# Row maxima of a softmax laid along all partitions by DMA and ScalarE instead of a TensorE transpose

## The chip, the core and the metric

The kernel runs on one core of a Trainium2 chip, in one launch. The metric is the device time of that core in microseconds, in several runs; beside it stands one execution taken by the hardware profiler. All data is float32.

## The reference, cut to what matters

```python
mod = (silu(c) @ wmod).reshape(8, 6, 1, 256)          # sa, ca, ga, sb, cb, gb by batch
h = layernorm(x) * (1 + ca) + sa                      # x: 8 batches x 1024 rows x 256
scores = einsum('nsd,ntd->nst', h * w_lhs, h * w_rhs) # 8 x 1024 x 1024
x = x + ga * (softmax(scores, axis=2) @ h)
h = layernorm(x) * (1 + cb) + sb
x = x + gb * (relu(h @ W1 + b1) @ W2 + b2)            # 256 -> 1024 -> 256
```

So each of eight batches has an attention over 1024 rows, whose softmax takes the maximum of every score row, and then a two-layer network on each row.

## The kernel before, in words

A batch's 1024 rows are eight tiles of 128 (P); i counts them, and a half g is four of them. The loop at the bottom runs over batches b and tiles i. One turn of it holds work of three places: the scores of the tile `ahead`, two tiles on; the softmax of the tile `late`, one tile on; and the product of tile i with the values, or a part of a product of two tiles. In the same turn stands a piece of the network of the batch before (half g = i // 4) and of the preparation of the next. `pin` ties each engine's instructions to the order in which the program emits them, DMAs included. So no scheduler moves anything, and each engine and each DMA queue runs strictly through its list.

Scores are symmetric in a way that the kernel uses: tile i computes only the columns from its own on (`direct`, L412), and ScalarE copies them from PSUM to the buffer sc (L419). The rest of the lower rows comes by `mirror`: VectorE turns blocks of 32x32 (L435), and `move` sends them to DRAM by four DMAs (D_m, L306) and reads them back by one (sc<-D_m, L309). Other transposes go the same way by `move`: the normalized rows of the next batch (D_a and X_a), of the network (D_f and X_f), and the network's result (D_y and Y). All of these are issued by SyncE, whose queue is in program order. A read stands there until its four writes have landed. The attention's and the network's products are done with seven half-size products for eight, which gives the sums on GpSimd and VectorE around them.

The transposed score tile is what the value product needs: columns of sc, with the score row along the free axis. So the maximum of each of the tile's 128 rows, which `row_max` leaves in one number per partition (m, L463), must stand along the free axis on every partition, as 128 x 128 numbers. `max_turn` does that by a TensorE transpose of m broadcast to 128 columns, into PSUM (pm, L468). `subtract` on VectorE (L475) takes pm from the columns, and `exponent` on ScalarE (L484) gives pT, the weights of the product. sc has one buffer, so a new batch's first scores wait for the last subtraction of the old one.

The network's first layer is made of pairs of column blocks, c = 0 to 3 for each half, two pairs in each turn with i % 4 < 2. `pair_products` (helper L726) writes pa, pb and pc, and ScalarE copies pa to kept (L747). Then `pair_sums` adds on VectorE, and `pair_last` writes a last product over the low half of pa (L778, through L726 too), adds it on VectorE (L779) and adds kept on GpSimd (L780). `pair_relu` is ScalarE's (L789, L790).

`max_turn` is called between matmuls, so that its small transpose stands inside another stage's stream. The turn i = 4 emits the next batch's second half before its maximum:

```python
                pair_last(fb, fg, c + 1)
                if i == 4:
                    if b + 1 < B:
                        prepare_blocks(b + 1, 1)
                        xg_times(b + 1, 1)
                    weights(*late)
                if ahead and ahead != extra:
                    row_max(*ahead)
```

Of the kernel before, what the change touches and what calls it, by code (L numbers as in the profile page):

```python
# [11 lines left out]
F32 = mybir.dt.float32  # L12
# [5 lines left out]
P = 128  # L18
# [6 lines left out]
def adaln_block_kernel(  # L25
# [13 lines left out]
    nc = tc.nc  # L39
    B, S, D = x.shape  # L40
    INTER = W1.shape[1]
    NT = S // P
# [3 lines left out]
    TH = HALF // P  # L46
    H2 = HALF // 2
    NH = NI // 2
    V = 32
    NV = P // V  # L50
    DX = D + 4

    const = ctx.enter_context(tc.tile_pool(name="const", bufs=1))
    two = ctx.enter_context(tc.tile_pool(name="two", bufs=2))
    work = ctx.enter_context(tc.tile_pool(name="work", bufs=3))
# [38 lines left out]
    early_d = two.tile([P, 4, D], F32, tag="X", name="early_d", bufs=1)  # L94
# [7 lines left out]
    def load_x0(q, queue):  # L102
# [11 lines left out]
        out=wv[ND : 2 * ND, :], in_=w_rhs.rearrange("a b (k p) -> (a b k) p", p=P)  # L114
# [19 lines left out]
    ident = const.tile([P, P], F32, name="ident")  # L134
# [5 lines left out]
    def warm(n):  # L140
# [9 lines left out]
            name=nc.get_next_instruction_name(),  # L150
# [6 lines left out]
    NC_ = ND * B  # L157
# [1 line left out]
        nc.tensor.transpose(pt_c[:, ts(k, B)], c_sb[:, ts(k, P)], ident[:B, :B])  # L159
    scT = const.tile([P, ND, B], F32, name="scT")  # L160
    scf = scT.rearrange("p k b -> p (k b)")
    den = const.tile([P, NC_], F32, name="den")
    nc.scalar.activation(den, pt_c[:, :NC_], AF.Exp, scale=-1.0)

    def silu():
# [90 lines left out]
    def prepare_start(b):  # L256
        xg_t[b] = two.tile([P, NT, DX], F32, tag="xg", name=f"xg_{b}")
        nc.gpsimd.memset(xg_t[b][:, :, D : D + 1], 1.0)
# [89 lines left out]
    def prepare_turn(b, g, vector=True):  # L348

        xg, pts = xg_t[b], []  # L350
        lT = lT_t[b, g] = two.tile([P, ND, HALF], F32, tag="lT", name=f"lT_{b}_{g}", bufs=2)
        rT = rT_t[b, g] = two.tile([P, ND, HALF], F32, tag="rT", name=f"rT_{b}_{g}", bufs=2)
        rows = lambda T, k: T[:, k, :].rearrange("p (t a v) -> p t a v", a=NV, v=V)
        for k in range(ND):
            if b > 0:
                pt = pre[b, g][:, k]
            else:
                pt = ps_t.tile([P, HALF], F32, tag="t", name=f"pth_{b}_{g}_{k}")
                for j in range(TH):
                    nc.tensor.transpose(pt[:, ts(j, P)], xg[:, g * TH + j, ts(k, P)], ident)  # L360
                pt = pt.rearrange("p (t a v) -> p t a v", a=NV, v=V)
            pts.append(pt)

        def left(k):
            nc.vector.tensor_scalar(
                rows(lT, k), pts[k], side_col(0, 0, k, b), side_col(0, 1, k, b),
                ALU.mult, ALU.add,
            )


        for k in range(ND):
            if vector:
                left(k)
            q = ND - 1 - k if vector else k
            nc.scalar.activation(
                rows(rT, q), pts[q], AF.Identity,
                scale=side_col(1, 0, q, b), bias=side_col(1, 1, q, b),
            )
        return left
# [13 lines left out]
    def score_row(b, i):  # L393
        if b == 0:
            return first_scores()[:, i].rearrange("p (n v) -> p n v", v=V)
        return sc_t[b].rearrange("p i a j v -> p j (i a) v")[:, i]
# [62 lines left out]
    max_t, pT_t = {}, {}  # L459

    def row_max(b, i):
        m = work.tile([P, 1], F32, tag="m", name=f"m_{b}_{i}")
        nc.vector.tensor_reduce(m, score_row(b, i), AX.XY, ALU.max)  # L463
        max_t[b, i] = m

    def max_turn(b, i):
        pm = ps_t.tile([P, HALF], F32, tag="t", name=f"pm_{b}_{i}")
        nc.tensor.transpose(pm[:, :P], max_t.pop((b, i)).to_broadcast([P, P]), ident)  # L468
        pT_t[b, i] = pm

    def subtract(b, i):

        pm = pT_t.pop((b, i))
        pT = work.tile([P, NT, P], F32, tag="pT", name=f"pT_{b}_{i}")
        nc.vector.tensor_tensor(  # L475
            pT.rearrange("p j (a v) -> p j a v", v=V),
            score_columns(b, i),
            pm[:, :P].rearrange("p (j a v) -> p j a v", j=1, v=V).to_broadcast([P, NT, NV, V]),
            ALU.subtract,
        )  # L480
        pT_t[b, i] = pT

    def exponent(b, i):
        nc.scalar.activation(pT_t[b, i], pT_t[b, i], AF.Exp)  # L484
# [35 lines left out]


    XS = D - P + 1
    tsum = const.tile([P, 4, TH, P + 4], F32, name="tsum")
    nc.gpsimd.memset(tsum[:, 1, :, P : P + 1], 1.0)

    def right_sums(b, which):

        xg = xg_t[b]
        b11, b12 = xg[:, 0:TH, P:D], xg[:, 0:TH, 0:P]
        b21, b22 = xg[:, TH:NT, P:D], xg[:, TH:NT, 0:P]  # L530
        t = [tsum[:, n, :, 0:P] for n in range(4)]
        ins = [(b12, b11), (b22, t[0]), (b22, b12), (t[1], b21)]
        for n in which:
            nc.gpsimd.tensor_tensor(t[n], *ins[n], ALU.subtract)
# [4 lines left out]
    def pair_begin(b, i, between=None):  # L539

        W = work.tile([P, 2, D + 4], F32, tag="W", name=f"W_{b}_{i}", bufs=1)
        pp = ps_a.tile([P, HALF], F32, tag="a", name=f"pp_{b}_{i}")
        one, other = halves(pT_t[b, i])
        rows = slice(P, P + XS)
        for out, lhs, h in (
            (pp[:, 0:XS], one, 0), (pp[:, XS : 2 * XS], other, 1)
        ):
            for t in range(TH):
                nc.tensor.matmul(  # L549
                    out, lhsT=lhs[:, t, :], rhs=xg_t[b][:, h * TH + t, P : P + XS],  # L550
                    start=(t == 0), stop=(t == TH - 1),
                )
            if between and h == 0:
                between()
        nc.scalar.copy(W[:, 1, rows], pp[:, 0:XS])
        two_t[b, i] = W, pp
# [22 lines left out]
    def pair_end(b, i):  # L579

        (s2, s4), (s3, a22) = halves(pT_t.pop((b, i))), halves(pT_t.pop((b, i + 1)))
        s1 = two_t.pop("s1")
        pq = ps_a.tile([P, HALF], F32, tag="a", name=f"pq_{b}_{i}")
        pr = ps_a.tile([P, HALF], F32, tag="a", name=f"pr_{b}_{i}")
        for out, lhs, rhs in (
            (pr[:, P : 2 * P], s1, tsum[:, 0, :, 0:P]),
            (pq[:, XS : XS + P], a22, tsum[:, 3, :, 0:P]),
            (pr[:, 2 * P : 3 * P], s3, tsum[:, 2, :, 0:P]),
            (pq[:, 0:XS], s2, tsum[:, 1, :, 0:XS]),
            (pr[:, 0:P], s4, xg_t[b][:, TH:NT, 0:P]),  # L590
        ):
            for t in range(TH):
                nc.tensor.matmul(  # L593
                    out, lhsT=lhs[:, t, :], rhs=rhs[:, t, :],
                    start=(t == 0), stop=(t == TH - 1),
                )
        two_t[b, i] = two_t[b, i][0], pq, pr
# [27 lines left out]
    def pair_stats(b, i):  # L625
        two_t.pop((b, i))
        for t in (i, i + 1):
            stats(mvb_of(b, t // TH), t % TH, x_tile(b, t), f"b{b}_{t}")
# [8 lines left out]
    def spare():  # L637
        if queue:
            queue.popleft()()
# [369 lines left out]
    def first_rows():  # L1009

        pr = ps_a.tile([P, HALF], F32, tag="a", name="prow")
        nc.tensor.matmul(
            pr[:, :HALF],
            lhsT=ident[:, 0:1].to_broadcast([P, P]),
            rhs=early_c[:, 0:2, :].rearrange("b j d -> b (j d)"),
            start=True,
            stop=True,
        )
        return pr
# [17 lines left out]
    pr = first_rows()  # L1037
# [106 lines left out]
    def weights(b, i):  # L1144
        subtract(b, i)
        exponent(b, i)

    last_exponent = (0, 1)
    late = None
    for b in range(B):  # L1150
        for i in range(NT):
# [8 lines left out]
            if (b, i) == (0, NT - 2):  # L1160

                prepare_turn(1, 1)
                product(b, i)
                direct(*ahead)
                exponent(*last_exponent)
                product_out(b, i)
                mirror(*ahead)
                early(b, i)
                for _ in range(4):
                    spare()  # L1170
                norms(b, i)
                row_max(*ahead)
                late, last_exponent = ahead, None
                continue
            if ahead and ahead != (0, 2):
                direct(*ahead)
            if b == 0:
# [37 lines left out]
            if first:  # L1215
# [28 lines left out]
                if (b, i) == (1, 0):  # L1244
                    exponent(*late)
                    late = None
# [41 lines left out]
            else:  # L1288
# [5 lines left out]
                if i == 2:  # L1294
                    left_sums(b, 1)
                elif i == 3:
                    pair_begin(b, i, turn_max)
                elif i == 6:
                    pair_begin(b, i, lambda: (max_turn(*late), weights(*late)))
                elif not ahead:  # L1300

                    pair_end(b, i - 1)
                    pair_out(b, i - 1)
                    pair_stats(b, i - 1)
# [64 lines left out]
            late = ahead if ahead != extra else None  # L1369
# [7 lines left out]
    b = B - 1  # L1377
# [74 lines left out]
```

## Time and profile before

| | before |
|---|---|
| time, median of 3 runs | 757.19 us (756.47 to 757.96) |
| profiled execution, its own time | 756.93 us |
| its span, first to last instruction | 755.1 us |
| busy: TensorE | 749.1 us, 99% |
| busy: VectorE | 574.9 us, 76% |
| busy: GpSimd | 570.9 us, 76% |
| busy: ScalarE | 374.9 us, 50% |
| DMA packets, bytes | 106213, 95.21 MB |
| maxima turned by TensorE (L468) | 64 times |

The page's first parts give each engine's busy time and the chain of work that ended last. Groups of instructions stand by line, engine and operation, with what ended the idle time before them. The timeline gives single instructions with start and duration in us: "PE" is a matmul on TensorE, "PEld" its weight load, "DVE" VectorE, "ACT" ScalarE, "POOL" GpSimd, and "SPq" a DMA that SyncE issues. The idle time before an instruction and what ended it stand in square brackets. L468 is line 468 of the kernel. A steady batch takes about 90.4 us.

### The profile page before, as it was taken

What the parts mean: (1) busy time and instruction counts of PE and PEld (TensorE: products, weight loads), DVE (VectorE), ACT (ScalarE), POOL (GpSimd) and SP (SyncE); (2) the same over time, 40 slices, a digit from 0 to 9 for tenths busy, and PEclk for the clock granted to TensorE, in tenths of its full rate; (3) what the DMA queues carried; (4) which work ended last, traced back from release to release, by engine and by line L of the source; (5) the groups of instructions that cost most, each with busy time, mean ns of one, the idle gap of its engine ahead of it and who ended that gap; (6) DMA issues with size and microseconds to landing.
All of it is one profiled execution on the core that took longest, in us unless ns stands there. A gap on an engine that the chain in (4) does not pass through costs nothing.

```text
span 755.1 us, 11883 instructions
## 1 busy us (share of the span) xinstructions
PE 749.1 (99%) x3876; PEld 623.4 (83%) x3876; DVE 574.9 (76%) x1259; ACT 374.9 (50%) x688; POOL 570.9 (76%) x658
## 2 busy tenths in 40 slices
PE   8999999999999999999999999999999999999998
PEld 4686889788897888888888878988889788888887
DVE  7787879778796879968878688876889777685632
ACT  4554646635375454745546444563546535252521
POOL 3762796878968798788877699777996888669741
PEclk9999999999999999999999999999999999999999
DMA  9033442455443453445534555245553354133220
GB/s 308 16 112 98 131 133 74 135 178 152 127 120 123 153 153 110 147 118 158 164 99 119 153 154 161 74 127 172 155 152 85 119 166 133 50 91 126 84 85 28
DMA packets 106213, 95.21 MB, mean 126 GB/s; under 512 B 29700, under 2 KB 98848, under 8 KB 106152
## 3 DMA queue, kind: packets, MB, share of 16 engines
q1 hardware_dynamic: 98408, 85.81, 38.6%
q10 hardware_dynamic: 7744, 8.65, 3.7%
q8 instruction: 30, 0.49, 0.3%
q14 instruction: 31, 0.25, 0.1%
HBM read 50.62 MB, written 43.81 MB: 125 GB/s over the span
## 4 chain that ended last, share of the span: by engine, by line
PE 96%; DMA 1%; DVE 1%; ACT 1%; issue 0%
PE psc L412 16%; PE pa L726 11%; PE po L501 10%; PE pr L593 7%; PE pb L726 7%; PE pc L726 7%; PE yc L806 6%; PE ya L806 6%; PE yb L806 6%; PE pq L593 5%; PE pp L549 5%; PE py L916 4%; PE yd L806 3%; DMA wm<-in_L_wmod_dram 1%; PE pm L468 1%; PE pmr L194 0%
## 5 line engine op out<-in xcount | busy, mean ns | idle before, releaser
L412 PE MATMUL psc<-rT,lT 128*128 128x512 f32 (+3 forms) x384 | 134.8, 487 | 0.0
L780 POOL TENSOR_TENSOR f<-f,kept 128x512 f32<-128x512 f32 x64 | 81.5, 1274 | 42.8 <-DVE f L779 20.1
L419 ACT COPY sc<-psc 128x512 f32<-128x512 f32 (+3 forms) x96 | 44.7, 476 | 119.9 <-PE psc L412 113.0
L484 ACT ACTIVATE pT<-pT 128x1024 f32<-128x1024 f32 x64 | 67.6, 1056 | 70.6 <-DVE pT L475 70.5
L475 DVE TENSOR_TENSOR pT<-sc,pm 128x1024 f32<-128x1024 f32 x64 | 77.3, 1208 | 29.3 <-PE pm L468 13.7
L412 PEld LDWEIGHTS psc<-rT,lT 128*128 128x128 f32 x384 | 66.4, 191 | 37.2 <-issue 25.6
L501 PE MATMUL po<-xg,pT 128*128 128x257 f32 x352 | 80.6, 380 | 0.0
L463 DVE TENSOR_REDUCE m<-sc 128x1 f32<-128x1024 f32 x64 | 77.4, 1209 | 2.2 <-ACT sc L419 1.8
L501 PEld LDWEIGHTS po<-xg,pT 128*128 128x128 f32 x352 | 66.2, 190 | 10.0 <-issue 0.7
L747 ACT COPY kept<-pa 128x512 f32<-128x512 f32 x64 | 37.4, 584 | 69.3 <-PE pa L726 69.1
L726 PE MATMUL pb<-hs,w1s 128*128 128x256 f32 x256 | 65.9, 380 | 0.1
L726 PE MATMUL pc<-hT,w 128*128 128x256 f32 x256 | 65.7, 379 | 0.0
L880 POOL TENSOR_TENSOR x<-x,Y 128x512 f32<-128x512 f32 x28 | 35.1, 1276 | 29.3 <-DMA Y<-D_y 29.3
L789 ACT ACTIVATE f<-f 128x512 f32<-128x512 f32 x64 | 39.8, 622 | 34.7 <-POOL f L780 34.7
L642 POOL TENSOR_TENSOR x<-x,rows 128x256 f32<-128x256 f32 x64 | 44.8, 732 | 13.8 <-ACT rows L1022 10.6
L726 PEld LDWEIGHTS pb<-hs,w1s 128*128 128x128 f32 x256 | 48.5, 190 | 7.3 <-DVE f L765 0.8
L726 PEld LDWEIGHTS pc<-hT,w 128*128 128x128 f32 x256 | 48.6, 190 | 6.7
L806 PE MATMUL yc<-f,w2s 128*128 128x256 f32 x224 | 51.3, 379 | 0.0
L435 DVE STREAM_TRANSPOSE Tm<-sc 128x896 f32<-128x896 f32 (+6 forms) x49 | 34.3, 701 | 20.3 <-ACT sc L419 19.6
L806 PEld LDWEIGHTS yc<-f,w2s 128*128 128x128 f32 x224 | 41.5, 190 | 8.1 <-issue 2.9
L549 PEld LDWEIGHTS pp<-xg,pT 128*128 128x128 f32 x336 | 41.9, 192 | 5.1 <-DVE st_b L241 1.4
L799 POOL TENSOR_TENSOR ft<-f 128x256 f32<-128x256 f32 x56 | 40.8, 729 | 6.8 <-ACT f L790 6.8
(166 smaller groups left out, 1821.1 us busy)
## 6 DMA issues: line engine op xcount, KB each, us to landing
D_f<-T_f SPq DMA_DIRECT2D x60, 128.0 KB, 2.5
X_f<-D_f SPq DMA_DIRECT2D x15, 512.0 KB, 3.7
D_a<-T_a SPq DMA_DIRECT2D x56, 128.0 KB, 2.8
D_y<-T_y SPq DMA_DIRECT2D x56, 128.0 KB, 2.9
Y<-D_y SPq DMA_DIRECT2D x14, 512.0 KB, 3.4
out_dram<-x SPq DMA_DIRECT2D x14, 512.0 KB, 4.4
X_a<-D_a SPq DMA_DIRECT2D x13, 512.0 KB, 3.4
x<-in_L_attn_x_dram ACTq DMA_DIRECT2D x12, 512.0 KB, 3.4
```

What stands on the lines that cost most here:

```text
L412: nc.tensor.matmul(psc[:, : hi - lo], lhsT=lT_t[b, i // TH][:, k, ts(i % TH, P)], rhs=rT_t[b, n][:, k, lo - n * HALF : HALF], start=(k == ...
L419: nc.scalar.copy(score_row(b, i)[:, lo // V : hi // V, :], psc[:, : hi - lo].rearrange("p (n v) -> p n v", v=V),)
L463: nc.vector.tensor_reduce(m, score_row(b, i), AX.XY, ALU.max)
L475: nc.vector.tensor_tensor(pT.rearrange("p j (a v) -> p j a v", v=V), score_columns(b, i), pm[:, :P].rearrange("p (j a v) -> p j a v", j=1, ...
L484: nc.scalar.activation(pT_t[b, i], pT_t[b, i], AF.Exp)
L501: nc.tensor.matmul(po[:, : D + 1], lhsT=pT[:, t, :], rhs=xg_t[b][:, t, 0 : D + 1], start=(t == 0), stop=(t == NT - 1),)
L549: nc.tensor.matmul(out, lhsT=lhs[:, t, :], rhs=xg_t[b][:, h * TH + t, P : P + XS], start=(t == 0), stop=(t == TH - 1),)
L593: nc.tensor.matmul(out, lhsT=lhs[:, t, :], rhs=rhs[:, t, :], start=(t == 0), stop=(t == TH - 1),)
L642: queue.append(lambda: nc.gpsimd.tensor_tensor(out, in0, row, op))
L726: nc.tensor.matmul(out, lhsT=lhsT, rhs=rhs, start=True, stop=True)
L780: nc.gpsimd.tensor_tensor(f[:, c::NH, hi], f[:, c::NH, hi], kept[:, None, hi].to_broadcast([P, 2, H2]), ALU.add,)
L806: nc.tensor.matmul(out, lhsT=lhs(c), rhs=rhs(c), start=(c == 0), stop=(c == NH - 1))
```

## The change

From the second batch on (b > 0), the maxima are spread without TensorE. Right after the maximum, `row_max` has VectorE turn m, broadcast to 32 columns, in blocks of 32x32 (mb, 128 x 32): the rows 0, 32, 64 and 96 of mb then hold 32 maxima each. Four DMAs issued by SyncE copy these rows, each from one partition to all 128, into mt (128 x 4 x 32, in SBUF). `max_turn` is a ScalarE copy of mt into the PSUM tile pm. mb and mt have one buffer each. For tile 7 the call of `max_turn` moves from inside `pair_begin` to the start of the turn i = 6, ahead of the next scores. To make room, xg's rows become two numbers shorter (DX), den lies in an early buffer, and the four parts of tsum are packed closer.

```diff
-    DX = D + 4
+    DX = D + 2
...
-    den = const.tile([P, NC_], F32, name="den")
+    den = early_d[:, 2, P : P + NC_]
...
         nc.vector.tensor_reduce(m, score_row(b, i), AX.XY, ALU.max)
         max_t[b, i] = m
+        if b == 0:
+            return
+
+
+        mb = work.tile([P, V], F32, tag="mb", name=f"mb_{b}_{i}", bufs=1)
+        nc.vector.transpose(mb, m.to_broadcast([P, V]))
+        mt = max_t[b, i] = work.tile([P, NV, V], F32, tag="mt", name=f"mt_{b}_{i}", bufs=1)
+        for a in range(NV):
+            nc.sync.dma_start(
+                out=mt[:, a],
+                in_=mb[a * V : a * V + 1].rearrange("o (n v) -> o n v", n=1).to_broadcast([1, P, V]),
+            )
 
     def max_turn(b, i):
+
         pm = ps_t.tile([P, HALF], F32, tag="t", name=f"pm_{b}_{i}")
-        nc.tensor.transpose(pm[:, :P], max_t.pop((b, i)).to_broadcast([P, P]), ident)
+        m = max_t.pop((b, i))
+        if b == 0:
+            nc.tensor.transpose(pm[:, :P], m.to_broadcast([P, P]), ident)
+        else:
+            nc.scalar.copy(pm[:, :P], m.rearrange("p a v -> p (a v)"))
         pT_t[b, i] = pm
...
-    tsum = const.tile([P, 4, TH, P + 4], F32, name="tsum")
-    nc.gpsimd.memset(tsum[:, 1, :, P : P + 1], 1.0)
+    tsum = const.tile([P, 4 * TH * P + TH * 4], F32, name="tsum")
+    tsum_first = tsum[:, : TH * (P + 4)].rearrange("p (t d) -> p t d", t=TH)
+    tsum_rest = tsum[:, TH * (P + 4) :].rearrange("p (n t d) -> p n t d", n=3, t=TH)
+    tsum_of = lambda n: tsum_first if n == 1 else tsum_rest[:, n - (n > 1)]
+    nc.gpsimd.memset(tsum_first[:, :, P : P + 1], 1.0)
...
+            if b > 0 and i == NT - 2:
+
+                max_turn(*late)
             if ahead and ahead != (0, 2):
                 direct(*ahead)
...
                 elif i == 6:
-                    pair_begin(b, i, lambda: (max_turn(*late), weights(*late)))
+                    pair_begin(b, i, lambda: weights(*late))
```

## The prediction

> **What bounds the kernel now.** The page first: part 1 (busy time of each engine) and part 4 (the chain that ended last).
>
> ```profile
> PE 749.1 (99%) x3876; PEld 623.4 (83%) x3876; DVE 574.9 (76%) x1259; ACT 374.9 (50%) x688; POOL 570.9 (76%) x658
> ...
> PE 96%; DMA 1%; DVE 1%; ACT 1%; issue 0%
> ```
>
> TensorE is busy 99% and is 96% of the chain. Read matmul by matmul, each one starts where the slot of the one before it ends (0.216 us for 256 columns, 0.11 us for 128), from 45 us to 674 us, without one gap over 0.15 us. So whatever leaves TensorE is a gain in full, and whatever makes TensorE wait once is a loss in full. The view of the tile pm shows what leaves:
>
> ```profile
> L468 PE MATMUL pm<-ident,m x64: 272/273/323, 24.6 to 681.7; 128*128 128x128 f32 x64
> ...
>   DVE pT L475: 13.7, 13
> ```
>
> The 273 ns are latency. What one transpose takes of TensorE is its slot, the distance to the next matmul's start: below, 492.53 to 492.64, 0.11 us.
>
> Next I looked for the place where the maxima's new way is tightest. In each batch I set the end of the maximum (L463) against the transpose (L468): in batches 1 to 6 between 3.8 and 10.5 us lie there, except for tile 6, where it is 2.48 us. So I took the timeline there, for batch 5, first SyncE alone, then TensorE and ScalarE.
>
> ```profile
> 485.63 2.99 SPq L306 DMA_DIRECT2D D_m<-Tm  x4
> 490.11 0.52 SPq L309 DMA_DIRECT2D sc<-D_m  x1
> 490.79 0.50 SPq L309 DMA_DIRECT2D Y<-D_y  x1
> 491.34 1.94 SPq L306 DMA_DIRECT2D D_a<-T_a  x4
> 496.50 0.34 SPq L309 DMA_DIRECT2D X_a<-D_a  x1
> ```
>
> ```profile
> 492.53 0.27 PE L468 MATMUL pm<-ident,m 128*128 128x128 f32 x1
> 492.64 0.60 PE L726 MATMUL pa<-hT,w1s 128*128 128x256 f32 x2
> ...
> 494.80 1.03 PE L726 MATMUL pc<-hT,w 128*128 128x256 f32 x4
> 495.66 0.59 PE L726 MATMUL pa<-hT,w1s 128*128 128x256 f32 x2
> ```
>
> ```profile
> 491.34 0.58 ACT L747 COPY kept<-pa 128x512 f32<-128x512 f32 x1
> 491.82 0.63 ACT L789 ACTIVATE f<-f 128x512 f32<-128x512 f32 x1
> 492.35 0.62 ACT L790 ACTIVATE f<-f 128x512 f32<-128x512 f32 x1
> 494.19 0.58 ACT L747 COPY kept<-pa 128x512 f32<-128x512 f32 x1 [1.22 <-PE pa L726]
> ```
>
> To be seen: SyncE's queue is in order and full. D_a's four writes end at 493.3, and the read X_a stands 3.2 us for them to land. On TensorE the matmul at 495.66 writes over pa, which the ScalarE copy kept of 494.19 must have read (L747 before L778): 0.9 us of slack there.
>
> **The change part by part.**
>
> *TensorE.* 56 of the 64 transposes go (batch 0 keeps its eight): 56 x 0.11 = 6.2 us, all on the path. Their weight loads lie beside matmuls, and 83% of PEld says no second limit shows up.
>
> *VectorE.* 56 block transposes of 128 x 32. The nearest row is STREAM_TRANSPOSE Tm 128x128, 0.27 us; a quarter of its size, so 0.1 to 0.27 us each. They sit right behind each maximum; VectorE is 76% busy. Cost zero, covered by the idle time beside it; without that cover 56 x 0.15 = 8 us.
>
> *SyncE.* 224 DMAs of 16 KB, 128 pieces of 128 bytes each, are put in program order behind the mirror's read and whatever else was queued. The same number and size of pieces has the mirror's smallest write, on the page of DMA issues:
>
> ```profile
> X_a<-D_a SPq DMA_DIRECT2D x13, 512.0 KB, 3.4
> ...
> D_m<-Tm SPq DMA_DIRECT2D x28, 16.0 KB, 1.9
> ```
>
> Issuing costs 0.48 us each (1.94 for four), landing 1.9 us; over all writes of that line from 1.5 to 6.5 us. That the source is a single partition is shown nowhere.
>
> *ScalarE.* 56 copies of 128x128 into PSUM, nearest row the copy sc<-psc 128x128, 0.24 us. It is their wait that counts: each holds up ScalarE's queue until four DMAs have landed.
>
> *Tile 6, batches 1 to 6: the wait.* In the changed program's order, SyncE has mt of tile 6 behind D_a and X_a, because the maximum is emitted after the next batch's blocks. ScalarE has its copy behind kept of pair 2 and ahead of two ReLUs, kept of pair 3, the exponentials and the sides rT and lT. In the times of batch 5: X_a ends at 496.84; four issues from 496.9, the last begins 3 x 0.48 later, 498.35; landing, which I take as 2.6 us because X_a's 512 KB, read just ahead in the same queue, is still under way (it lands 3.4 us after its own issue, 499.9), gives 500.95. Copy and handing over 0.3: 501.25. ReLUs 1.15: 502.4. kept 0.58: 503.0. Then the matmul of 495.66 may start, which without the transposes of tiles 5 and 6 would have been ready at 495.45. TensorE stands 7.5 us. Batch 5 has X_a 3.97 us after pm; in batches 1 to 6 that distance is 3.66, 2.78, 2.38, 2.66, 3.97 and 4.33, mean 3.30, so the mean stall is 6.85 us, and six of them are 41 us. With landing at 1.5 us it is 5.75 (34 us), with 4.0 us 8.25 (50 us). VectorE's subtraction waits with it, and behind that the sums of pair 3 (1.6 us, from 502.5); the next matmuls, po of tile 5, need neither. The ReLUs of pairs 2 and 3, the sides and tile 7 then move by less than TensorE does.
>
> *The clock.* TensorE now never rests, so nothing shows a rest in the middle. What the trace shows is both ends: the timeline's first matmuls, and the windows view of the tail (its PEclk is the third number from the end).
>
> ```profile
> 1.45 2.07 PE L143 MATMUL pw<-early_a 128*128 128x512 f32 x2 [1.45 <-DVE early_a L131]
> ...
> 6.62 2.03 PE L194 MATMUL pmr<-wm,scT 128*8 128x512 f32 x4
> ...
> 752.00:755.10 3.10, 0.00 (x0) 0.00 (x0) 0.30 (x1) 0.00 (x0) 0.00 (x0) 0.90 0.12 42
> ```
>
> Two matmuls of 512 columns take 2.07 us at the start, four take 2.03 from 6.62 on: half speed for some 5.2 us. After the last matmul (751.9) the mean grant of 0.90 means half clock in the last 0.6 us: it fell 2.6 us after the rest began. The Trainium skill, "TensorE: Matmul & The Clock Gate", section "Why this matters for your kernels", says the same against this change: no rests over about 3 us between bursts, one idle window (3.4 us) brings the half clock, and about 3.4 us of work brings it back. By the trace's start, a stall of 7 us costs 5.2 / 2 = 2.6 us more, by the skill's 3.4 us 1.7, and nothing if the clock holds. I take 2.0, since the start's matmuls were not dense: 6 x 2.0 = 12 us.
>
> *The other tiles.* Tile 7 is moved ahead of ScalarE's score copies. In batch 4 its subtraction started at 413.84, held by the transpose at 413.46; the maximum ended at 408.44, so the DMAs land by 408.6 + 1.45 + 2.2 = 412.3 and the subtraction may go up to a microsecond earlier. That matters, since the copies of the next scores wait for it (they overwrite sc). It pays for tile 0, whose four issues (1.9 us) now stand before D_f and X_f: net X_f about 1 us later. The additions on hs (L714) start 2.2 to 4.0 us ahead of the first pa, and no matmul waited even with 2.2. So zero, at most 1 us a batch. Tile 3: mt is behind the read sc at 458.88, lands near 463.7 instead of the transpose at 461.61, so the subtraction is about 1.9 us late; its use at 470.93 is far, but VectorE passes about 1 us on to tile 5. There the copy goes in front of Y's scaling, and kept of pair 1 (483.07, needed at 484.60) ends some 1.4 us later: 0.4 us of stall in six batches, 2.5 us. Batch 7 has no D_a; its tiles 6 and 7 are late by about 1.5 us together. Tiles 1, 2 and 4 have 1.5 us and more in hand. The narrower DX, the new places of tsum and den move bytes, no instructions: zero, at most 1 us either way.
>
> *The sum*, against the profiled execution's own 756.93 us (span 755.1; the median of the runs is 757.19, 0.3 above it): 756.9 - 6.2 + 41 + 12 + 2.5 + 1.5 = 807.7 us, or 808. The measurement can tell about 0.2% (1.5 us) from no change.
>
> **The rivals.**
>
> *The clock holds.* TensorE stands, but is granted full speed after. 807.7 - 12 = 796 us. For it: the fall took 2.6 us at the tail, so a stall under 3 us would pass. Against: the stalls are 5.75 us and more.
>
> *One partition is a slow source.* All 128 pieces of each DMA come out of one partition; if four then land 2.5 us later than taken, tile 6 costs 6 x 2.5 = 15 us more, and tiles 0, 3 and 5, without slack left, about 2 us each in seven batches, 40 us: some 860 us. Against: pieces of 128 bytes in the mirror's smallest write are cheap[...].
>
> *Faster: every copy finds its row landed.* Then only the 6.2 us are left, 750.7 us. The point it hangs on is tile 6: kept of pair 3 must end by 495.45, so the four DMAs must have landed by 495.45 - 0.58 - 1.15 - 0.3 = 493.4. The maximum ends at 490.05; issued at once they would land at 490.2 + 1.45 + 1.9 = 493.55, just about in time. It is the place behind X_a alone, 496.9 instead of 490.2, that decides. For it there is only a queue that runs 6.7 us earlier in the changed kernel, and nothing of D_y, D_m or D_a is taken out of it.
>
> **How the numbers follow.** The forecast (stalls at tile 6, with the clock) 0.70, 785 to 830 with the bounds of landing and clock; the clock holds 0.15 (796); the slow source 0.10 (860); faster 0.04 (751); no change, by gains and small stalls that cancel, 0.01. Range 785 to 832: it leaves out the slow source and the faster case. Faster 0.04, same 0.01, slower 0.95.
>
> **What would show it.** Right: six gaps of 5 to 9 us on TensorE, one in each batch from 1 to 6, before pa<-hT,w1s (line 746 with the diff's lines counted in), ended by ACT kept; ScalarE's copy pm<-mt waiting for DMA, 56 times, longest at tile 6; mt's issue right behind X_a's; the clock row with half-speed stretches; 56 fewer pm matmuls. Wrong: TensorE without gaps (then the queue ran ahead), gaps at tiles 0, 3 and 5 as long as at 6 (slow source), or long gaps with a full clock.

## The result, and the profile after

The changed kernel is slower by 14%: 862.34 us median of 4 runs (856.98 to 865.27) against 757.03 us of 4 runs of before. The ratio is 1.138, its 95% interval 1.133 to 1.144. The forecast of 808 us had the right sign, named the right place, and was 54 us short; the result lies outside its range of 785 to 832 us. The profiled execution took 865.27 us, with a span of 863.5 us.

The page of the changed kernel, parts 1, 2, 4 and 5:

```profile
PE 780.5 (90%) x3820; PEld 638.6 (74%) x3820; DVE 580.0 (67%) x1315; ACT 387.7 (45%) x744; POOL 567.3 (66%) x658
...
PEclk9999997999989999899988999979999899999999
...
PE 13%; DVE 3%; ACT 1%; DMA 1%; issue 1%; POOL 1%; SPq 1%; DVEq 0%; ACTq 0%; POOLq 0%
...
L746 PE MATMUL pa<-hT,w1s 128*128 128x256 f32 x128 | 44.6, 436 | 67.1 <-ACT kept L767 67.1
L485 ACT COPY pm<-mt 128x128 f32<-128x128 f32 x56 | 15.1, 270 | 195.6 <-DMA mt<-mb 195.5
L518 PE MATMUL po<-xg,pT 128*128 128x257 f32 x352 | 95.8, 431 | 3.0 <-DVE m L463 3.0
```

TensorE has 56 instructions less and is busy 31 us longer. Behind the second bar of a group stands the idle time of its engine before it: 67.1 us of TensorE before pa<-hT,w1s, all ended by ScalarE's kept, and 195.5 us of ScalarE before its copies, ended by the DMAs. The matmuls po lasted 380 ns before and 431 ns now: some of them ran at half speed, which is also the digits below 9 in PEclk. (The chain of part 4 covers only a fifth of the span here, and I don't use it.)

The view of the tile mt, the new one:

```profile
L473 SPq DMA_DIRECT2D mt<-mb x224: 469/600/1569, 70.6 to 788.6; - x112
L485 ACT COPY pm<-mt x56: 269/269/275, 75.8 to 791.3; 128x128 f32<-128x128 f32 x56
...
  ACT pm L485: 195.5, 52
...
DMA to landing us min/median/max: 2.4/2.7/4.1
```

One issue is 0.60 us, and one DMA lands 2.7 us after its own issue. The four are issued one after the other, 0.64 us apart (median), so the copy starts 4.5 us or more (median 4.7 us) after the first one's start.

The timeline of batch 4, all engines in one answer, cut to SyncE, ScalarE and the matmul that waits. It shows both long waits of a batch:

```profile
443.20 2.51 SPq L473 DMA_DIRECT2D mt<-mb  x4
...
447.86 0.27 ACT L485 COPY pm<-mt 128x128 f32<-128x128 f32 x1 [6.38 <-DMA mt<-mb]
448.06 1.51 ACT L877 ACTIVATE Y<-Y,gcol 128x512 f32<-128x512 f32 x2
...
449.90 0.57 ACT L767 COPY kept<-pa 128x512 f32<-128x512 f32 x1
...
450.52 1.22 PE L746 MATMUL pa<-hT,w1s 128*128 128x256 f32 x2 [3.81 <-ACT kept L767]
...
456.61 0.21 DVE L470 STREAM_TRANSPOSE mb<-m 128x32 f32<-128x32 f32 x1
...
456.99 0.55 SPq L309 DMA_DIRECT2D sc<-D_m  x1
...
458.25 1.93 SPq L306 DMA_DIRECT2D D_a<-T_a  x4
...
463.16 0.34 SPq L309 DMA_DIRECT2D X_a<-D_a  x1
...
463.55 2.57 SPq L473 DMA_DIRECT2D mt<-mb  x4
...
468.38 0.27 ACT L485 COPY pm<-mt 128x128 f32<-128x128 f32 x1 [8.25 <-DMA mt<-mb]
468.59 0.62 ACT L809 ACTIVATE f<-f 128x512 f32<-128x512 f32 x1
469.12 0.61 ACT L810 ACTIVATE f<-f 128x512 f32<-128x512 f32 x1
469.64 0.57 ACT L767 COPY kept<-pa 128x512 f32<-128x512 f32 x1
...
470.26 1.22 PE L746 MATMUL pa<-hT,w1s 128*128 128x256 f32 x2 [6.00 <-ACT kept L767]
```

Read the second half first, it is tile 6. The row is turned at 456.6, but its DMAs stand in SyncE's queue behind D_a and X_a and are issued only at 463.55. ScalarE's copy waits for them until 468.38, two ReLUs and kept follow, and TensorE stands 6.0 us. The first half is tile 5: there the copy waits until 447.86, Y's scaling and kept of pair 1 are behind it, and TensorE stands 3.8 us.

The windows view of the same place, from the gap at tile 6 on (columns: window, its length, then busy time of PE, PEld, DVE, ACT, POOL, then PEclk):

```profile
464.00:469.40 5.40, 0.26 (x2) 0.00 (x0) 0.66 (x1) 1.01 (x3) 1.51 (x2) 1.00 0.63 208
469.40:472.80 3.40, 2.54 (x6) 2.09 (x7) 3.09 (x7) 3.40 (x6) 2.83 (x5) 0.51 0.00 0
472.80:476.20 3.40, 3.40 (x9) 2.66 (x9) 0.83 (x2) 3.26 (x6) 2.29 (x4) 0.50 0.04 8
476.20:480.00 3.80, 3.80 (x12) 2.21 (x12) 2.41 (x9) 0.27 (x1) 3.56 (x6) 0.99 0.06 11
```

The granted clock falls to a half at 469.4, while TensorE still stands, and is full again only at 476.2. TensorE is back at work from 470.26, so for some six microseconds it works at half speed.

To add all this up I took every matmul's start from 20 us on and compared its distance to the next start with the slot of its size (0.216 us for 256 columns and so on). What is over is a gap, or, where it is about one slot, a matmul at half clock. The sum of the slots fell by 6.5 us, half clock costs 27.8 us more than before, gaps 87.1 us more: together 108.4 us, as the spans differ. The split between the last two columns is good to some 2 us, since a short gap can look like a matmul at half clock: the kernel without DMAs shows 1.7 us, and no half clock while it works. The same count for the runs below:

| kernel | median us | ratio to before (95%) | gaps us | half clock us |
|---|---|---|---|---|
| before | 757.0 | | 2.9 | 0.4 |
| changed | 862.3 | 1.138 (1.133 to 1.144) | 90.0 | 28.2 |
| tile 6 by TensorE | 814.5 | 1.075 (1.072 to 1.079) | 51.6 | 16.9 |
| tiles 5 and 6 by TensorE | 783.7 | 1.037 (1.033 to 1.041) | 28.4 | 5.6 |
| tile 6's maximum ahead | 821.7 | 1.085 (1.083 to 1.088) | 55.8 | 17.7 |
| tile 6's copy behind | 851.5 | 1.123 (1.121 to 1.125) | 77.8 | 26.7 |
| two DMAs a tile | 820.4 | 1.082 (1.079 to 1.085) | 58.1 | 16.8 |
| source spread | 840.4 | 1.109 (1.108 to 1.111) | 72.4 | 20.1 |
| DMAs that nobody reads | 777.8 | 1.027 (1.026 to 1.029) | 21.4 | 2.0 |
| no DMAs | 756.8 | 0.999 (0.998 to 1.000) | 9.7 | 1.7 |

### The profile page after: what moved, and what is told of

It reads as the page before. It is cut to its first block, busy times and chain, and to the rows that moved or that the text cites. A ratio compares the mean times of both kernels' runs of the same rounds, so it can differ in the third digit from the quotient of the medians.

```text
span 863.5 us, 12361 instructions
## 1 busy us (share of the span) xinstructions
PE 780.5 (90%) x3820; PEld 638.6 (74%) x3820; DVE 580.0 (67%) x1315; ACT 387.7 (45%) x744; POOL 567.3 (66%) x658
## 5 line engine op out<-in xcount | busy, mean ns | idle before, releaser
L800 POOL TENSOR_TENSOR f<-f,kept 128x512 f32<-128x512 f32 x64 | 81.4, 1271 | 54.0 <-DVE rs L277 25.3
L746 PE MATMUL pa<-hT,w1s 128*128 128x256 f32 x128 | 44.6, 436 | 67.1 <-ACT kept L767 67.1
L485 ACT COPY pm<-mt 128x128 f32<-128x128 f32 x56 | 15.1, 270 | 195.6 <-DMA mt<-mb 195.5
L518 PE MATMUL po<-xg,pT 128*128 128x257 f32 x352 | 95.8, 431 | 3.0 <-DVE m L463 3.0
L518 PEld LDWEIGHTS po<-xg,pT 128*128 128x128 f32 x352 | 77.4, 222 | 18.7 <-ACT pT L501 3.4
L746 PEld LDWEIGHTS pa<-hT,w1s 128*128 128x128 f32 x128 | 24.4, 205 | 77.4 <-ACT kept L767 75.1
L734 POOL TENSOR_TENSOR hs<-hT 128x256 f32<-128x256 f32 x16 | 11.6, 727 | 87.2 <-DVE hT L725 87.2
```

What stands on the lines that cost most here:

```text
L518: nc.tensor.matmul(po[:, : D + 1], lhsT=pT[:, t, :], rhs=xg_t[b][:, t, 0 : D + 1], start=(t == 0), stop=(t == NT - 1),)
L746: nc.tensor.matmul(out, lhsT=lhsT, rhs=rhs, start=True, stop=True)
L800: nc.gpsimd.tensor_tensor(f[:, c::NH, hi], f[:, c::NH, hi], kept[:, None, hi].to_broadcast([P, 2, H2]), ALU.add,)
```

## Experiments: where the 105 us are

**Tile 6 by TensorE.** A tuple BY_DMA holds the seven other tiles.

```
-        if b == 0:
+        if b == 0 or i not in BY_DMA:
```

> Tile 6 of each batch gets its maxima by TensorE as before, the other seven by DMA. Theory (tile 6's place behind D_a and X_a in SyncE's queue, with the copy ahead of kept of pair 3): its gaps of 4.9 to 8.3 us go, 37.6 us in all, and about half of the 28 us lost at half clock, so about 862 - 38 - 14 = 810 us, with tile 5's gaps of 4 us still there. Rival (the wait moves to the next tile, since the sum of DMA times is what bounds): above 845 us, tile 7's or tile 5's gaps grow by as much.

814.53 us. The long gaps behind tile 5's are gone, tile 5's of 3.0 to 4.5 us stay where they were. Tile 6 thus costs 48 us of the 105: 37.5 us of gaps (8.3, 5.4, 5.8, 6.2, 7.0 and 4.9) and its share of the half clock.

**Tiles 5 and 6 by TensorE.**

> Tiles 5 and 6 of each batch by TensorE, the other six by DMA. Theory (tile 5's copy stands ahead of kept of pair 1 and waits some 4 us): beside tile 6's 38 us and half its clock loss, tile 5's 21 us and the rest of the clock loss go: 814.5 - 21 - 9 = about 785 us; what is left is tiles 1, 2 and the last batch. Rival (a batch has a fixed excess of DMA time, and the gaps reappear at tiles 0 to 4 and 7): above 800 us.

783.66 us, as the theory had it. Tile 5 costs another 31 us. Now 27 us are left, and they are of another kind (below).

**Tile 6's place in SyncE's queue.** The maximum of tile 6, with the turn and the four DMAs, goes ahead of the transposes that D_a and X_a wait for. No instruction is added or removed.

```
                 if i == 4:
-                    if b + 1 < B:
-                        prepare_blocks(b + 1, 1)
-                        xg_times(b + 1, 1)
                     weights(*late)
                 if ahead and ahead != extra:
                     row_max(*ahead)
+                if i == 4 and b + 1 < B:
+                    prepare_blocks(b + 1, 1)
+                    xg_times(b + 1, 1)
```

> At tile 5's turn VectorE does the subtraction, tile 6's maximum and the turn first and then the T_a transposes, so that tile 6's four DMAs stand in SyncE's queue ahead of the four D_a and X_a in place of behind them. Theory (the place in the queue makes tile 6 the worst): mt of tile 6 is issued some 5 us earlier, its gaps fall from 4.9 to 8.3 us to under 2 us, X_a comes 2.5 to 4 us later but is read only behind exp of tile 6: about 862 - 27 - 12 = 823 us. Rival (SyncE's four issues of 2.5 us only change who waits): X_a becomes late, ScalarE's rT and TensorE's psc<-rT,lT get gaps of 3 to 5 us, 850 us or more.

821.71 us. From the maximum's end to the first issue are now 1.4 to 3.3 us in batches 1 to 6, where it had been 5.4 to 8.1 us. The timeline of batch 4 shows both what is gained and what is late next:

```profile
435.96 2.41 SPq L473 DMA_DIRECT2D mt<-mb  x4
...
438.40 2.20 SPq L306 DMA_DIRECT2D D_a<-T_a  x4
...
440.56 0.27 ACT L485 COPY pm<-mt 128x128 f32<-128x128 f32 x1 [3.41 <-DMA mt<-mb]
...
442.44 0.70 PE L746 MATMUL pa<-hT,w1s 128*128 128x256 f32 x2 [1.16 <-ACT kept L767]
...
446.92 1.52 ACT L342 ACTIVATE rT<-X_a,sides 128x512 f32<-128x512 f32 x2 [3.58 <-DMA X_a<-D_a]
```

TensorE's gap is 1.2 us instead of 6.0. ScalarE now waits 3.6 us for X_a, but in a place where TensorE has other work. So of tile 6's 48 us, 41 are the place and not the four DMAs as such. Most of it is the place in SyncE's queue (1.4 to 3.3 us in place of 5.4 to 8.1); a smaller part is VectorE's order, for the maximum itself also comes 0.6 to 2.3 us earlier against the matmul that waits.

**Tile 6's copy behind kept of pair 3.** The DMAs stay where they were; ScalarE's copy and VectorE's subtraction are put behind the last product of pair 3.

```
-                if late and i != 4 and (b, i) != (1, 0):
+                if late and i not in (4, 5) and (b, i) != (1, 0):
                     subtract(*late)
                 pair_products(fb, fg, c + 1, ...)
+                if i == 5:
+                    turn_max()
+                    subtract(*late)
```

> All DMAs as in the changed kernel and where they were in SyncE's queue; for tile 6 alone ScalarE's copy and VectorE's subtraction come after the last product of pair 3, so kept of pair 3 no longer stands behind the copy. Theory (head of line on ScalarE, not the landing as such): tile 6's six gaps of 4.9 to 8.3 us before pa<-hT,w1s fall under 1.5 us each, no new gap of that size at po<-xg,pT since 16 matmuls of tile 5 and psc lie between, half of the clock loss goes: about 862 - 33 - 12 = 817 us. Rival (the late row itself is what TensorE waits for): gaps move to po<-xg,pT or psc<-rT,lT with the same size, 850 us or more.

851.5 us, the rival's number. Waits of the kernel with the copy behind:

```profile
PE pa L746 <- ACT kept L767: 27.1, 10, 4.5
...
PE ya L826 <- ACT Y L838: 20.1, 7, 3.9
...
PE psc L412 <- ACT rT L342: 11.5, 6, 4.2
```

Of the 67.1 us before pa, 27.1 are left, those of the other tiles. But 20.1 us before ya (2.7 us in the changed kernel) and 11.5 us before psc (none there) have come. ScalarE executes in order, so whatever stands behind the copy waits until the row is there: earlier it was kept, now rT and Y. My theory, that it was only the wrong instruction that stood behind the copy, fell. What has to be mended is when the row arrives.

**Two of the four DMAs.** The loop runs over two pieces, and the copy writes them twice.

```
-        for a in range(NV):
+        for a in range(2):
```

> The changed kernel with two of the four DMAs for each tile; ScalarE's copy writes the two pieces twice (half of the columns get other columns' maxima and the exponent is scaled, so not the true softmax). Theory (issue in order, 0.60 us each, then a landing of 2.7 us): first issue to last landing falls from 4.6 to 3.3 us, so each of some 18 gaps gets 1.3 us shorter, and later loads come 1.3 us earlier a tile: 862 - 23 - 8 = about 830 us. Rival (the landing and the place in the queue set the wait, the number of pieces little): 850 us or more.

820.37 us, 42 us less, more than expected, and not where it was expected. Tile 6's gaps are still 4.7 to 7.3 us; at tile 5 they fell from about 4 us to between 0.2 and 3.4 us, and at tile 2 none over 0.3 us is left. Landing stayed at 2.8 us. This fits a wait that at tile 6 is decided by the place behind X_a, and at the other tiles by the time that four issues keep SyncE.

**Is one partition a slow source?** Each destination partition is fed from its own partition.

```
-                in_=mb[a * V : a * V + 1].rearrange("o (n v) -> o n v", n=1).to_broadcast([1, P, V]),
+                in_=mb,
```

> Same DMAs in number, size and place, but each destination partition is fed from its own partition in place of one partition for all 32; the maxima are replaced by a constant and the exponent scaled, so the softmax is not the true one. Theory (issue in order and fixed landing time): landing stays near 2.7 us, issue near 0.60 us, time within 6 us of the changed kernel's, 856 to 868 us. Rival (one partition is a slow source): landing falls to about the 1.9 us of D_m, each of about 18 stalls gets some 0.8 us shorter, and with the clock the time falls to 845 us or below.

840.44 us. The tile's view, with its landing time:

```profile
L475 SPq DMA_DIRECT2D mt<-mb x224: 464/600/1419, 71.5 to 764.5; - x112
...
DMA to landing us min/median/max: 1.7/2.2/3.9
```

The issue time is the same, so 0.60 us doesn't come from the single partition. Landing is 0.5 us shorter, and 22 us go with it. The rival was right in kind: one partition as the source is slower, by 0.5 us and not by the 2.5 us that the prediction's rival had set.

**DMAs that nobody reads.** TensorE transposes the maxima as before, and the turn and four DMAs are made as well.

```
+        mt = work.tile([P, NV, V], F32, ...)        # written, never read
...
-            nc.scalar.copy(pm[:, :P], m.rearrange("p a v -> p (a v)"))
+            nc.tensor.transpose(pm[:, :P], m.to_broadcast([P, P]), ident)
```

> Turn and four DMAs are issued as in the changed kernel, but TensorE transposes the maxima as before and nothing reads the rows that the DMAs bring. Theory (the copies' wait on ScalarE is what costs): 757 to 763 us, only what 56 VectorE turns and 224 issues on SyncE's queue, about 0.6 us each, do to the loads behind them. Rival (the DMAs themselves hold up the X_a and y loads or use up the queue's or the rings' time): 785 us or more, with gaps ended by DMAs.

777.82 us, 15 to 20 us above the theory and below the rival's 785: the DMAs cost 20 us without any reader. The timeline in tile 2's turn shows one way:

```profile
446.13 2.56 SPq L473 DMA_DIRECT2D mt<-mb  x4
...
448.73 2.99 SPq L306 DMA_DIRECT2D D_y<-T_y  x4
...
457.36 2.50 POOL L897 TENSOR_TENSOR x<-x,Y 128x512 f32<-128x512 f32 x2 [2.73 <-DMA Y<-D_y]
...
461.12 0.63 ACT L806 ACTIVATE f<-f 128x512 f32<-128x512 f32 x1 [2.39 <-POOL f L797]
...
462.80 0.60 ACT L764 COPY kept<-pa 128x512 f32<-128x512 f32 x1
...
463.45 0.70 PE L743 MATMUL pa<-hT,w1s 128*128 128x256 f32 x2 [2.29 <-ACT kept L764]
```

The four issues, which are tile 1's, take 2.56 us of SyncE, and D_y's writes start right behind them. GpSimd's addition on x waits for the read Y, and through f, the ReLUs and kept it reaches TensorE. These gaps at tile 2 are 1.0, 1.9, 1.6, 2.4 and 1.5 us in batches 2 to 6, 8.4 us in all, and in the changed kernel 1.0, 1.7, 2.5, 1.7 and 1.4, 8.3 us. The changed kernel's timeline has the same chain in batch 4, with tile 1's four issues ended and D_y's begun at 396.28:

```profile
405.95 2.50 POOL L900 TENSOR_TENSOR x<-x,Y 128x512 f32<-128x512 f32 x2 [3.27 <-DMA Y<-D_y]
...
409.71 0.63 ACT L809 ACTIVATE f<-f 128x512 f32<-128x512 f32 x1 [2.93 <-POOL f L800]
...
412.04 0.70 PE L746 MATMUL pa<-hT,w1s 128*128 128x256 f32 x2 [2.29 <-ACT kept L767]
```

So tile 2's gaps there do not come from a copy that waits. (Another part of the 20 us is this kernel's own: VectorE's next turn waits 18.1 us in 8 places, because mb has one buffer and the DMAs are still reading it. In the changed kernel that is 0.7 us.)

## Experiments: where the saving went

**No DMAs.** The copies read a constant tile. The text below says that the turn is gone too; in fact its 56 instructions were still made.

```
-        mt = max_t[b, i] = work.tile(...)
-        for a in range(NV): nc.sync.dma_start(...)
+        max_t[b, i] = flat
```

> Leaves out the true softmax maxima: the VectorE turn and the four DMAs are gone, ScalarE's copies read a constant tile, and the exponent is scaled so that it stays finite; every other edit of the change is kept. Theory (the loss is all in waiting for the DMAs): the 56 TensorE transposes saved come out as they were summed, 56 x 0.11 = 6.2 us, so about 751 us, no gap over 1 us at pa<-hT,w1s and full granted clock. Rival (the ScalarE copies in front of the ReLUs and of kept, or the new order of the other instructions, cost time by themselves): over 757 us.

756.80 us (754.64 to 758.77): not the theory's 751 but next to the rival's 757, although the matmuls' slots are 6.1 us less. Gaps of 0.2 to 1.4 us have appeared, above all before ya<-ft,w2s. Without any waiting for DMAs the change gains nothing that can be told from zero. Seven further runs looked for the reason.

**The same without the turn.**

> As the kernel without the four DMAs (constant maxima, scaled exponent, so not the true softmax; ScalarE's copies kept), but without VectorE's 56 turns of 0.21 us too. That kernel took 756.8 us. If the turn is what took the saving back (12 us on VectorE): about 751 us. If TensorE's earlier demand or the copies did: 755 to 757.5 us.

756.45 us (753.41 to 759.29), ratio 0.999 (0.998 to 1.000). The turn is not it, as predicted at zero.

**The edits of layout alone** (DX, den, tsum; maxima by TensorE, nothing else).

> The change's smaller edits alone: the two columns less in the blocks, den inside early_d, tsum split in two; maxima all by TensorE, no turn, no copy, no DMA. As they were costed, nothing: 756.5 to 758 us. If the new places in SBUF or the strides cost something: 759 us or more, and this is then part of what the kernel without DMAs did not gain.

757.35 us, ratio 1.0002 (0.9993 to 1.0011). Zero, as predicted.

**TensorE shorter, nothing else.** The kernel before, with one step of po left out:

```
-        for t in [t for p in parts for t in range(p * TH, (p + 1) * TH)]:
+        for t in [t for p in parts for t in range(p * TH, (p + 1) * TH) if b == 0 or t != TH]:
```

> The kernel before with one of the eight steps of each product po left out from the second batch on (so that part of the sum is missing): 28 matmul instructions of 0.217 us, 6.1 us less for TensorE, as much as the transposes saved, and no other edit. Theory A (what TensorE saves here is waited for elsewhere): 755.5 to 757.5 us, with new gaps at ya<-ft,w2s or the like. Theory B (the saving is real in this kernel, and the change's copies or order took it back): 751 to 752.5 us, without gaps.

751.63 us, ratio 0.993 (0.991 to 0.994). So a saving of 6.1 us on TensorE is worth 5.6 us in this kernel. The prediction's "a gain in full" was nearly right; something in the change takes it back.

**The copies.** Maxima by TensorE, tile 7's call in its new place, and beside each transpose a ScalarE copy of 128 columns that nobody needs; the second kernel is the same without the copies.

```
         nc.tensor.transpose(pm[:, :P], m.to_broadcast([P, P]), ident)
+        if b > 0:
+            nc.scalar.copy(pm[:, P : 2 * P], flat.rearrange("p a v -> p (a v)"))
```

> All maxima by TensorE, the layout edits, tile 7's call in its new, earlier place, and beside each transpose a ScalarE copy of 128 columns from a constant tile into unused columns of the same PSUM tile, where the changed kernel has its copy; no turn, no DMA. If the copies take back what the transposes save: about 757 + 5 = 762 us, with gaps at ya<-ft,w2s. If they hide: within 1 us of the same kernel without them.

> The same without the copies: all maxima by TensorE, layout edits, tile 7's call in its earlier place. If the earlier place alone is what costs: 760 us or more, with the gaps at ya<-ft,w2s; if not: 757 to 758 us.

763.23 us with the copies, ratio 1.008 (1.007 to 1.010); 757.76 us without, ratio 1.0008 (1.0002 to 1.0015), so the earlier place of tile 7's call costs some 0.6 us. A copy in this place of ScalarE's order costs 5.5 us over 56, 0.1 us each, though ScalarE is busy only half the time. The gaps are again before ya<-ft,w2s (2.8 us of them). One reservation: here the copy also waits for its transpose, since both write one tile, as this kernel's waits show:

```profile
ACT pm L479 <- PE pm L477: 52.9, 49, 1.5
```

So the 5.5 us is the price of a copy with that wait. That the copy alone takes the whole 6 us in the kernel without DMAs fits (757 - 6 + 5.5 = 756.5) and nothing else is left of the change, but it was not isolated.

**The copies taken away.** An earlier try at the same question: the subtraction reads the constant tile from SBUF.

```
-            nc.scalar.copy(pm[:, :P], m.rearrange("p a v -> p (a v)"))
+            pm = m.rearrange("p a v -> p (a v)")
```

> As the kernel without the four DMAs (constant maxima and a scaled exponent, so not the true softmax; VectorE's turn still made), but ScalarE's 56 copies of 0.27 us are gone too: the subtraction reads the constant from SBUF. That kernel took 756.8 us where 751 was summed. Theory A (TensorE's shorter work meets GpSimd's ft before it is ready, so what the transposes save is waited for at ya<-ft,w2s): again 756 to 757 us, with 4 us or more at ya<-ft,w2s. Theory B (the copies stand in ScalarE's order and delay what TensorE waits for): about 752 us, with the gaps at ya<-ft,w2s gone.

763.79 us, ratio 1.008 (1.006 to 1.011): neither theory. The groups of VectorE and of GpSimd in this kernel:

```profile
L489 DVE TENSOR_TENSOR pT<-sc,flat 128x1024 f32<-128x1024 f32 x56 | 78.2, 1396 | 14.9 <-DMA sc<-D_m 14.8
```

```profile
L797 POOL TENSOR_TENSOR f<-f,kept 128x512 f32<-128x512 f32 x64 | 94.3, 1474 | 31.8 <-DVE f L796 16.0 <-DVE rs L277 7.2 <-ACT xg L281 4.6
...
L816 POOL TENSOR_TENSOR ft<-f 128x256 f32<-128x256 f32 x56 | 50.0, 892 | 0.9 <-ACT f L807 0.9
```

With the copies these were 1207, 1276 and 731 ns. A subtraction with both inputs in SBUF makes itself and GpSimd's work slower: GpSimd is busy 619 us instead of 567. So the run says nothing on the copies' own price. It shows what they spare: with the rows read directly from SBUF this kernel took 763.79 us, with the copies 756.80.

**Shorter turns.** The kernel before with matmuls of 32 columns in place of the transposes:

> The kernel before with one edit: from the second batch on the 56 transposes of the maxima are matmuls with 32 columns in place of 128 (the maxima of the other columns are left out and the exponent is scaled, so not the true softmax); no copy, no DMA, no VectorE turn, no other order. TensorE saves about 56 x 0.05 to 0.08 = 3 to 4.5 us by itself. Theory A (what TensorE saves here is waited for elsewhere, at ya<-ft,w2s): 756.5 to 757.5 us, gaps there. Theory B (the saving is real, and the change's copies and turns took it back): 753 to 754.5 us, no new gaps.

764.08 us, 6.5 us slower. My edit had made the work longer: an ordinary f32 matmul is two instructions here and the transpose was one.

```profile
L472 PE MATMUL pm<-ident,m x112: 192/236/277, 77.6 to 687.9; 128*128 128x32 f32 x112
```

So nothing on the two theories; the step of po replaced it.

**Only tiles in hidden places.**

> The changed kernel with only tiles 1 and 4 by DMA, the two without a gap of their own; the other six by TensorE. Theory (in hidden places the DMA way saves its transposes and costs nothing): 14 x 0.11 = 1.5 us less, 755.7 us, if the saving can be kept at all; 757 if it cannot. Rival (even these tiles' DMAs delay later loads on SyncE's queue): 760 us or more.

> Tiles 1, 4 and 7 by DMA, the other five by TensorE. Theory: as with 1 and 4, but for 3 us in the last batch before ya<-ft,w2s: 757 to 760 us. Rival (tile 7's early copy and its DMAs delay pair work): 764 us or more.

759.59 us (ratio 1.0024, 1.0014 to 1.0034) with tiles 1 and 4, 767.42 us (1.012, 1.011 to 1.014) with tile 7 as well. Both lie above their theory's number, the second at its rival's, with 8 and 17 us of gaps in small pieces: tile 7 is not hidden, and tiles 1 and 4 cost 2 us instead of saving 1.5. Two of these gaps, 0.8 and 1.1 us with tiles 1 and 4 alone, are again those in tile 2's turn. No selection of tiles that I ran is faster than the kernel before.

## Why the prediction was wrong, step by step

The sum came out 57.6 us short in the profiled executions (50.8 predicted, 108.4 measured). The steps that failed are tile 5, the clock and tile 2, in this order of size; tile 6 held.

| step | predicted us | measured us |
|---|---|---|
| transposes | -6.2 | -6.5 in slots |
| tile 6, gaps | 41 | 37.5 |
| tile 5, gaps | 2.5 | 21.3, and 3.3 just ahead before pb |
| tile 2, gaps | 0 | 8.3 |
| batch 7, gaps | 1.5 | 6.2 |
| others | 0 | about 10, the 2.9 of before taken off: 3.1 before the first po, 1.5 before pp, the rest small; their cause stays open |
| half clock | 12 | 27.8 |

*Right.* Tile 6 was the largest cost, for the reason given: mt behind D_a and X_a, the copy ahead of kept. Moving the maximum ahead took 41 us away and tile 6 by TensorE 48. That 41 and 37.5 us lie so close is in part luck. From the first issue to the waiting matmul it took 6.6 to 6.7 us (taken: 6.1), and in batches 2 to 6, behind tile 5's stall, TensorE came there 6.6 to 7.8 us after the maximum (taken: 5.4): two errors against each other. The clock did not hold, and nothing was hidden. The slow source is real but worth 22 us. That its number, 860 us, lies beside the measured 862 is chance: the landing grew by 0.5 us and not by 2.5, and tiles 0 and 3 have no such gaps.

*Wrong: tile 5 was taken to be 0.4 us a batch.* It is 4 us in five batches. The step said that the copy stands in front of Y's scaling and that kept of pair 1 ends 1.4 us later. The order was right, the arrival was not. I had read it in batch 5 of before, where the read sc starts as the maximum ends, so that four issues could follow half a microsecond behind it. These are that batch's maximum, its read sc and the matmul that needs kept of pair 1:

```profile
474.66 1.21 DVE L463 TENSOR_REDUCE m<-sc 128x1 f32<-128x1024 f32 x1
...
475.83 0.53 SPq L309 DMA_DIRECT2D sc<-D_m  x1
...
484.60 0.59 PE L726 MATMUL pa<-hT,w1s 128*128 128x256 f32 x2
```

Already in the other batches of before this read starts up to 2.1 us behind the maximum. In batch 4 of the changed kernel it is 2.6 us, and mt stands behind it (443.20 in the timeline above), for sc waits in SyncE until D_m has landed:

```profile
438.75 1.21 DVE L463 TENSOR_REDUCE m<-sc 128x1 f32<-128x1024 f32 x1
...
442.56 0.55 SPq L309 DMA_DIRECT2D sc<-D_m  x1
```

In these five batches the first mt of tile 5 is issued 3.0 to 4.0 us after the maximum, and the copy starts some 4.7 us after that (taken: about 3.7, from an issue of 0.48 us, measured 0.60, and a landing of 2.2, measured 2.7). And the maximum itself comes later against TensorE: 8.7 us ahead of the waiting matmul before, 6.6 us now, a shift of 2.1 us where I had allowed 1. With a slack of 1 us at kept of pair 1, all that came through in full.

*Wrong: tile 2 at zero.* I had looked whether its row was in time, and it was. I had not followed the queue past the four issues: D_y and Y stand behind those of tile 1, and GpSimd waits for Y. So a row that is in time can still cost a gap one tile later. The kernel with unread DMAs shows it by itself, 8.4 us.

*Wrong: the clock at 6 x 2.0 us.* The price of one fall was nearly right: 27.8 us over 12 stretches of half clock is 2.3 us each. There are twelve and not six, since five of tile 5's gaps and the 3.1 us before the first po bring one each. The Trainium skill says in "TensorE: Matmul & The Clock Gate", section "What's actually happening", that the activity window of 3413 ns is free-running (the 3.4 us of the prediction stand there too). The trace agrees: all twelve stretches begin on one grid of 3.41 us and last 3.41, 6.83 or 10.24 us. It also shows what I had not taken from it: a gap of about 4 us need not contain a whole idle window. The fall at 449.0 came behind a window, 445.6 to 449.0, in which TensorE had still worked for 1.1 us (the windows view, columns as above):

```profile
445.59:449.00 3.41, 1.13 (x6) 0.65 (x4) 0.10 (x1) 1.14 (x3) 1.23 (x1) 0.99 0.09 16
```

Counted in slots, each of the twelve falls comes behind a window of the grid with at most 1.2 us of matmuls in it, and none comes behind a window with 1.4 us or more. So a gap of 4 us can cost as much clock as one of 7, and how it lies on the grid counts beside its length.

*Wrong: the copies at zero beside their wait.* The saving of 6.2 us is real on TensorE, but the kernel without DMAs has none of it. The 5.5 us that needless copies cost in the same place make them the likely taker. This step hid behind the large ones. It means that with the copies where they stand, no better arrangement of the DMAs alone would have made this change pay: with no DMA at all it only reaches the time of before. (Issuing the DMAs from another engine's queue was not tried.)

## What to carry to other kernels

Time for a value that comes by DMA is not its transfer but its place: the wait of the queue's earlier entries, then the issues one after the other, then the landing, here 0.3 to 8 us, 2.5 us and 2.7 us; and the issues must be counted a second time for the loads that come behind them. An engine that waits in order for such a value stops everything behind it, so changing which instruction stands there moves the gap more than it removes it (11 us less here, of 105). Before building on a saving, take the new mechanism's costs away one by one and see whether the saving is there at all: here it was not.

## What the runs showed of the hardware that I had not expected

- Half clock comes in whole stretches of 3.41 us on a fixed grid; one fall costs about 2.3 us of TensorE, and gaps of 3.1 to 4.7 us were enough in 6 of the 12 cases. By an estimate from the slots, what decides is the work inside one window of the grid. In the eight traces here that fell, at most 1.37 us stood in the window before a fall, and at least 1.37 us in every other window at full clock between 20 us and the last matmul: about 40% of the 3.41 us.
- Four DMAs of 16 KB with 128-byte pieces keep SyncE 2.5 us, 0.60 us each, whether their source is one partition or 128; one partition as the source adds 0.5 us to the landing (2.7 against 2.2 us).
- A VectorE subtraction with both inputs in SBUF took 1396 ns instead of 1207, and GpSimd's f and ft beside it grew by 15 and 22%. The Trainium skill, "SBUF — State Buffer", section "Who interferes with whom", names a cause that fits: such an instruction and a GpSimd one that reads SBUF contend for a read port that they share. With one input in PSUM, as in both kernels, f took 1274 ns (before) and 1271 ns (changed).
- A ScalarE copy of 0.27 us in a half idle ScalarE still cost 0.1 us of the kernel's time each, in the run in which it also waits for its transpose.
